# Row maxima of a graph-attention layer gathered and spread by ScalarE copies between partition quarters instead of two TensorE products

## The chip, the core and the metric

The kernel runs on one core of a Trainium2 chip. The core's engines are TensorE (PE: products, and PEld: the loading of their stationary operand), VectorE (DVE), ScalarE (ACT), GpSimd (POOL) and SyncE (SP, which here only issues transfers). Each engine works through its own queue in order; a semaphore holds an instruction until what it needs from another engine is done. The metric is the device time of one execution in microseconds, as the median of the runs.

## The reference

Four graph layers, each followed by a residual sum and a layer norm over the 256 features, on 4096 nodes with a dense 4096 x 4096 matrix `adj`. Layer 0 is masked attention with 4 heads, layers 2 and 3 are normalized products with `adj`. The change lies in layer 1:

```python
Wh = x @ W
e_src = Wh @ a[:d_out]
e_dst = Wh @ a[d_out:]
e = jax.nn.leaky_relu(e_src[:, None] + e_dst[None, :], 0.2)
mask = (adj > 0) | jnp.eye(N, dtype=bool)
e = jnp.where(mask, e, NEG_INF)
alpha = jax.nn.softmax(e, axis=1)
h = alpha @ Wh
x = _layernorm(x + h)
```

For the softmax of a row, the maximum of the row's e is subtracted before the exponential. Since leaky_relu grows with its argument, the maximum of e follows from the maximum of e_dst over the unmasked columns: it is leaky_relu(e_src + that maximum).

## The kernel before

Layer 0 ends near 1440 us; layer 1 runs from there to 1953 us, and layers 2 and 3 follow. Layer 1 takes the rows in 32 units of 128, and each unit in four steps s = 0 to 3 of 32 rows (`NSB` = 4, `QB` = 32). To use all 128 partitions for 32 rows, the 4096 columns are split in `NA` = 4 quarters of 1024 (`QK`): partition a*32 + i holds row i and columns of quarter a. A step works on tiles of 128 x 1024.

The class `Unit` holds what is done for 128 rows:

- `__init__` issues SyncE's loads of the mask (`mk`, two tiles of bfloat16, in a ring of seven) and makes the small tiles `mx` (maxima) and `nm` (the negated, leaky row maximum, the bias of the exponential), each 128 x 4, two buffers. `eq` is e_src, spread to all quarters beforehand.
- `score(s)` (L709, L711), on VectorE: the mask becomes 0 or a large negative number, and one fused instruction adds e_dst (`ed_b`) into z and leaves the maximum of each partition in a column of `mx`. An extra small instruction writes that column.
- `leaky(s)` (L724), on ScalarE: adds e_src and applies the leaky slope, in place.
- `turn_max` and `spread_max`: each row's maximum is spread over four partitions, one per quarter. L730 transposes `mx` on TensorE, L732 takes the maximum over the quarters on VectorE, L739 repeats it four times; L744 turns it back by a product with the identity, and L752 and L755 make `nm`.
- `expo(s)` (L758), on ScalarE: exp(z + nm), in place.
- `turn(s)` (L765), on VectorE: transposes z in 32 x 32 blocks into `pt`, which has two buffers, one per unit.
- `attend(s)` (L775), on TensorE: 16 products of 128 columns of alpha with the matching 128 rows of `wh` (256 features and a column of ones, whose product is the softmax's sum). Each product takes 32 rows of each of the four steps, so a unit's first product needs all four of its `turn`s.
- `finish` (L785, L787 and the layer norm's statistics L113, L114), on VectorE: divides by the sum and adds to the residual row.

The order within each engine's queue is written out by hand in `gat_step(t)`, called for t = 0 to 139. In step t stand, in this order: `score(t)`; where t is a multiple of 4, `turn_max` of the unit that `score` finished in step t-1; `attend(t-10)`; `turn(t-6)`; `spread_max` of the same unit as `turn_max`; `leaky(t)`; `expo(t-5)`; and `finish` of the unit whose last `attend` was in step t-1. So `turn_max` stands in TensorE's queue ahead of the 16 products of that step, and `spread_max` behind them. On VectorE the two halves stand on either side of a `turn`.

The first steps also carry the rest of the projection: `project_w(t+2)` for t = 0 to 5 (16 products, L137, into two PSUM buffers, each emptied by a ScalarE copy, L145), and in step 5 the spreading of e_src of the later rows (`take_es`, L148, then `spread_es`).

Of the kernel before, what the change touches and what calls it, by code (L numbers as in the profile page):

```python
# [8 lines left out]
F32 = mybir.dt.float32  # L9
BF16 = mybir.dt.bfloat16  # L10
AF = mybir.ActivationFunctionType
ALU = mybir.AluOpType
AX = mybir.AxisListType
# [3 lines left out]
P = 128  # L17
# [12 lines left out]
NA = 4  # L30
QB = P // NA
QK = N // NA
NBK = QK // QB
NSB = P // QB
# [6 lines left out]
SLOPE = 0.2  # L41
# [3 lines left out]
def tile_gnn(  # L45
# [18 lines left out]
    nc = tc.nc  # L64
# [10 lines left out]
    ident = const.tile([P, P], F32, name="ident")  # L75
# [35 lines left out]
    def ln_stats(pool, row, ci):  # L111
        st = pool.tile([P, 6], F32, tag="bnst", name="bnst")
        nc.vector.bn_stats(st, row)  # L113
        nc.vector.bn_aggr(mv[:, ci, :], st)  # L114
# [54 lines left out]
    with ExitStack() as l0:  # L169
        ps_t = l0.enter_context(tc.tile_pool(name="l0ps_t", bufs=1, space=PSUM))  # L170
        ps_o = l0.enter_context(tc.tile_pool(name="l0ps_o", bufs=1, space=PSUM))
# [4 lines left out]
        wk = l0.enter_context(tc.tile_pool(name="l0work", bufs=1))  # L176
# [503 lines left out]
    with ExitStack() as l1:  # L680
        wk = l1.enter_context(tc.tile_pool(name="l1work", bufs=2))
        pp_ = l1.enter_context(tc.tile_pool(name="l1pt", bufs=2))
        ps_o = l1.enter_context(tc.tile_pool(name="l1ps_o", bufs=2, space=PSUM))

        class Unit:


            def __init__(self, u):
                self.u = u
                self.z = [None] * NSB  # L690
                self.mk = []
                for half in range(2):
                    mk = bp.tile([P, 2, QK], BF16, tag="bias", name="mk1")
                    i0 = u * P + half * 2 * QB
                    for a in range(NA):
                        nc.sync.dma_start(
                            mk[a * QB : (a + 1) * QB, :, :],
                            edge[i0 : i0 + 2 * QB, a * QK : (a + 1) * QK].rearrange(
                                "(s i) m -> i s m", i=QB
                            ),  # L700
                        )
                    self.mk += [mk[:, 0, :], mk[:, 1, :]]
                self.mx = wk.tile([P, NSB], F32, tag="mx", name="mx")
                self.nm = wk.tile([P, NSB], F32, tag="nm", name="nm")
                self.eq = es_q.rearrange("p a b -> p (a b)")[:, u * NSB : (u + 1) * NSB]

            def score(self, s):
                m = self.mk[s]
                nc.vector.tensor_scalar(m, m, 0.0, MASK1, ALU.is_le, ALU.mult)  # L709
                z = zp.tile([P, QK], F32, tag="z", name="z1")  # L710
                nc.vector.tensor_tensor_reduce(  # L711
                    z,
                    m,
                    ed_b,
                    1.0,
                    NEG,
                    ALU.add,
                    ALU.max,
                    self.mx[:, s : s + 1],
                )  # L720
                self.z[s] = z

            def leaky(self, s):
                nc.scalar.activation(  # L724
                    self.z[s], self.z[s], AF.Prelu, bias=self.eq[:, s : s + 1], alpha=SLOPE
                )

            def turn_max(self):
                pm = ps_o.tile([P, 512], F32, tag="pm", name="pm")
                nc.tensor.transpose(pm[0:NSB, 0:P], self.mx, ident)  # L730
                mr = wk.tile([NSB, QB], F32, tag="mr", name="mr")
                nc.vector.tensor_reduce(  # L732
                    mr,
                    pm[0:NSB, 0:P].rearrange("s (a i) -> s i a", i=QB),
                    AX.X,
                    ALU.max,
                )
                self.mr = wk.tile([NSB, NA, QB], F32, tag="mr4", name="mr4")
                nc.vector.tensor_copy(self.mr, mr.unsqueeze(1).to_broadcast([NSB, NA, QB]))  # L739

            def spread_max(self):

                pm = ps_o.tile([P, 512], F32, tag="pm", name="pm2")
                nc.tensor.matmul(  # L744
                    pm[:, 0:NSB],
                    self.mr.rearrange("s a i -> s (a i)"),
                    ident[0:NSB, 0:NSB],
                    start=True,
                    stop=True,
                )  # L750
                ne = wk.tile([P, NSB], F32, tag="ne", name="ne")
                nc.vector.scalar_tensor_tensor(  # L752
                    ne, pm[:, 0:NSB], -1.0, self.eq, ALU.mult, ALU.subtract
                )
                nc.vector.scalar_tensor_tensor(self.nm, ne, SLOPE, ne, ALU.mult, ALU.min)  # L755

            def expo(self, s):
                nc.scalar.activation(  # L758
                    self.z[s], self.z[s], AF.Exp, bias=self.nm[:, s : s + 1]
                )  # L760

            def turn(self, s):
                if s == 0:
                    self.pt = pp_.tile([P, NBK, NSB, QB], F32, tag="pt", name="pt")
                nc.vector.transpose(  # L765
                    self.pt[:, :, s, :], self.z[s].rearrange("p (b r) -> p b r", r=QB)
                )
                self.z[s] = None

            def attend(self, s):  # L770
                if s == 0:
                    self.po = ps_o.tile([P, 512], F32, tag="po", name="po")
                n = NBK // NSB
                for b in range(s * n, (s + 1) * n):
                    nc.tensor.matmul(  # L775
                        self.po[:, 0 : D + 1],
                        self.pt[:, b, :, :].rearrange("p s i -> p (s i)"),
                        wh[:, b, :],
                        start=(b == 0),
                        stop=(b == NBK - 1),  # L780
                    )

            def finish(self):
                rc = wk.tile([P, 1], F32, tag="rc", name="rc")
                nc.vector.reciprocal(rc, self.po[:, D : D + 1])  # L785
                row = xc[:, self.u, :]
                nc.vector.scalar_tensor_tensor(  # L787
                    row, self.po[:, 0:D], rc, row, ALU.mult, ALU.add
                )
                ln_stats(wk, row, self.u)  # L790

        units = {}
        n_t = NCH * NSB

        def at(t):
            u, s = divmod(t, NSB)
            return (units[u], s) if 0 <= t < n_t else (None, s)

        def gat_step(t):
            if 0 <= t < n_t and t % NSB == 0:  # L800
                units[t // NSB] = Unit(t // NSB)
            u, s = at(t)
            if u:
                u.score(s)
            u, s = at(t - NSB)
            if u and s == 0:
                u.turn_max()
            u, s = at(t - NSB - 6)
            if u:
                u.attend(s)  # L810
            u, s = at(t - NSB - 2)
            if u:
                u.turn(s)
            u, s = at(t - NSB)
            if u and s == 0:
                u.spread_max()
            u, s = at(t)
            if u:
                u.leaky(s)
            u, s = at(t - NSB - 1)  # L820
            if u:
                u.expo(s)
            u, s = at(t - NSB - 7)
            if u and s == NSB - 1:
                u.finish()
                del units[u.u]

        with tc.manual_schedule():
            for t in range(n_t + NSB + 8):
                gat_step(t)  # L830
                if t + 2 < NJ:
                    project_w(t + 2)
                if t + 3 == NJ:
                    take_es(2 * NSB, NBK)
                    spread_es(2 * NSB, NBK, ps_o.tile([P, 512], F32, tag="pm", name="pe"))

                    for j in range(NJ):
                        nc.sync.dma_start(
                            xc.rearrange("p (a j) e -> p a j e", j=NJ)[:, :, j, :],
                            x0.rearrange("(a j p) e -> p a j e", p=P, j=NJ)[:, :, j, :],  # L840
                        )
                    nc.vector.reciprocal(d3, d3)
                    nc.vector.reciprocal(d2, d2)
                    nc.vector.tensor_scalar(sel, sel, -1.0, 1.0, ALU.mult, ALU.add)
                    nc.vector.tensor_tensor(d2, d2, sel, ALU.mult)
# [4 lines left out]
    with ExitStack() as l2:  # L850
# [3 lines left out]
        wk = l2.enter_context(tc.tile_pool(name="l2work", bufs=3))  # L854
# [169 lines left out]
        with tc.manual_schedule():  # L1024
# [4 lines left out]
            for t in range(n_all):  # L1029
# [16 lines left out]
                if c == NP - 1:  # L1046
# [8 lines left out]
                    for s in range(NSJ):  # L1055
                        p = jb * NSJ + s
# [65 lines left out]
```

## Time and profile before

| | us |
|---|---|
| median of 3 runs (2809.99 to 2813.46) | 2810.7 |
| the profiled execution, its own time | 2810.3 |
| its span in the trace | 2808.5 |
| TensorE busy in the span | 2740.4 (98%) |
| VectorE busy | 2234.3 (80%) |
| ScalarE busy | 1615.1 (58%) |
| first attention product of layer 1 (L775) starts at | 1485.5 |
| last one starts at | 1951.9 |

The span is what the trace covers; the run's own time has some 2 us around it. All trace times are counted from the span's start. Of the small instructions on the maxima, each of L730, L732, L739, L752 and L755 occurs 32 times; L744 appears 64 times, as two passes for each product. Their mean durations: L730 272 ns, L732 274 ns, L739 216 ns, L744 258 ns, L752 159 ns, L755 161 ns. A busy time of TensorE is not the same as its full pace: products are pipelined, and one of 379 ns follows the one before by less than that.

### The profile page before, as it was taken

Reading aid. Unit: us, or ns where it says so; the run is one execution under the profiler, and the core shown is the slowest. Engines: PE = TensorE matmul, PEld = TensorE weight load, DVE = VectorE, ACT = ScalarE, POOL = GpSimd, SP = SyncE. Lnnn points to the kernel's source line nnn. Section 1 sums busy time; section 2 is a strip of 40 time slices with the busy share of each in tenths; the row PEclk is TensorE's granted clock in tenths of the full one; section 3 lists DMA queues with packets and bytes.
Section 4 is the critical chain, followed back from the end, with each engine's and each line's share of the span. In section 5 each row is a group of like instructions: output and inputs, shape, how many; then the busy total and the mean of one; then the engine's idle time right before and its main releaser. Section 6 shows DMA issues by size and latency. Waiting matters only on the chain.

```text
span 2808.5 us, 58032 instructions
## 1 busy us (share of the span) xinstructions
PE 2740.4 (98%) x23664; PEld 1870.2 (67%) x23664; DVE 2234.3 (80%) x4091; ACT 1615.1 (58%) x2483; POOL 234.2 (8%) x404
## 2 busy tenths in 40 slices
PE   6999999999999999999998999999999999999997
PEld 4677777777777777777777888887444444444443
DVE  4799999999898999999758888885876568666565
ACT  2699999999999999999855655653100001000000
POOL 1111111111111111111100000000200000000000
PEclk9999999999999999999998999999999999999999
DMA  6344444444444444444362222212555545555552
GB/s 157 61 86 85 87 92 85 88 86 88 90 87 82 90 91 82 86 92 89 100 188 68 76 73 70 76 46 72 177 157 173 163 154 163 164 160 179 180 169 76
DMA packets 671291, 308.01 MB, mean 110 GB/s; under 512 B 547376, under 2 KB 577456, under 8 KB 671024
## 3 DMA queue, kind: packets, MB, share of 16 engines
q1 hardware_dynamic: 655776, 265.10, 38.4%
q0 software_dynamic: 13440, 37.77, 3.5%
q8 instruction: 185, 3.03, 0.5%
q10 hardware_dynamic: 1808, 1.44, 0.2%
q14 instruction: 82, 0.67, 0.1%
HBM read 258.21 MB, written 46.01 MB: 108 GB/s over the span
## 4 chain that ended last, share of the span: by engine, by line
PE 96%; DVE 2%; ACT 1%; DMA 1%; issue 1%; SPq 0%; DVEq 0%; ACTq 0%
PE m L950 27%; PE po L423 17%; PE po L775 16%; PE sc L366 16%; PE ptr L405 10%; PE py L984 2%; PE pq L313 1%; PE pp L335 1%; PE pb L441 1%; PE pk L210 1%; PE pv L226 1%; PE sc L137 1%; PE pm L744 0%; SPq L256 0%; DMA xt<-in_xT 0%
## 5 line engine op out<-in xcount | busy, mean ns | idle before, releaser
L375 DVE CUSTOM_DVE_ANT_0 z<-sc,bias 128x1024 f32<-128x1024 f32 x512 | 605.8, 1220 | 40.5 <-PE sc L366 38.9
L391 ACT ACTIVATE z<-z,nm 128x1024 f32<-128x1024 f32 x512 | 590.2, 1153 | 6.7 <-DVE nm L387 6.7
L413 ACT COPY pt<-ptr 128x1024 f32<-128x1024 f32 x507 | 511.3, 1008 | 99.2 <-PE ptr L405 89.3
L366 PE MATMUL sc<-store,qT 64*128 64x512 f32 x2048 | 507.0, 608 | 1.4 <-DVE mx L375 1.3
L423 PE MATMUL po<-pt,xc 128*64 128x128 f32 x8192 | 504.1, 276 | 0.0
L775 PE MATMUL po<-store,pt 128*128 128x257 f32 x2048 | 459.5, 382 | 3.6 <-DVE pt L765 3.6
L423 PEld LDWEIGHTS po<-pt,xc 128*64 128x64 f32 x8192 | 442.1, 137 | 17.6 <-DVE pt L411 0.2
L405 PEld LDWEIGHTS ptr<-ident,z 64*128 64x128 f32 x8192 | 322.3, 138 | 177.6 <-issue 78.4
L775 PEld LDWEIGHTS po<-store,pt 128*128 128x128 f32 x2048 | 385.0, 190 | 62.9 <-issue 3.6
L950 PE MATMUL m<-asum,ysum 128*128 128x512 f32 x768 | 357.0, 595 | 6.3 <-issue 6.3
L405 PE MATMUL ptr<-ident,z 64*128 64x64 f32 x8192 | 356.5, 225 | 5.8 <-ACT pt L413 4.4
L366 PEld LDWEIGHTS sc<-store,qT 64*128 64x128 f32 x2048 | 192.9, 189 | 119.7 <-issue 109.4
L950 PEld LDWEIGHTS m<-asum,ysum 128*128 128x128 f32 x768 | 146.1, 190 | 177.9 <-issue 160.2
L950 PE MATMUL m<-asum,store 128*128 128x512 f32 x512 | 263.1, 596 | 0.0
L724 ACT ACTIVATE z<-z,es_q 128x1024 f32<-128x1024 f32 x128 | 147.1, 1149 | 183.2 <-DVE mx L711 178.9
L950 PE MATMUL m<-a,ysum 128*128 128x512 f32 x512 | 245.3, 592 | 0.0
L295 POOL DMA_DIRECT2D edge<-mk x256 | 145.3, 568 | 1004.5 <-ACT mk L289 981.0
L956 ACT COPY e<-m 128x512 f32<-128x512 f32 x32 | 18.5, 586 | 351.3 <-PE m L950 351.3
L919 DVE TENSOR_TENSOR asum<-a 128x512 f32<-128x512 f32 x128 | 88.0, 687 | 163.7 <-PE m L950 163.7
L278 DVE SCALAR_TENSOR_TENSOR bias<-rt,gb,u 128x512 f32<-128x512 f32 x256 | 194.1, 758 | 9.1
L950 PEld LDWEIGHTS m<-asum,store 128*128 128x128 f32 x512 | 97.8, 191 | 123.6 <-issue 121.9
L272 DVE STREAM_TRANSPOSE rt<-raw 128x512 f32<-128x512 f32 x256 | 179.6, 702 | 0.0
(126 smaller groups left out, 2544.5 us busy)
## 6 DMA issues: line engine op xcount, KB each, us to landing
a<-in_adjT SPq DMA_DIRECT2D x256, 512.0 KB, 5.1
raw<-in_adjT SPq DMA_DIRECT2D x512, 128.0 KB, 3.9
edge<-mk POOLq DMA_DIRECT2D x256, 128.0 KB, 2.5
mk<-edge SPq DMA_DIRECT2D x256, 128.0 KB, 2.9
xt<-in_xT SPq DMA_DIRECT2D x8, 512.0 KB, 5.3
xq<-in_xT SPq DMA_DIRECT2D x32, 128.0 KB, 3.8
xr<-in_x SPq DMA_DIRECT2D x32, 128.0 KB, 3.0
x<-xs POOLq DMA_DIRECT2D x8, 512.0 KB, 4.0
```

The source lines that it names most:

```text
L272: nc.vector.transpose(rt.rearrange("p (b r) -> p b r", r=QB), self.raw_now[:, half * nb : (half + 1) * nb, :],)
L278: nc.vector.scalar_tensor_tensor(self.bias[k][:, m0 : m0 + HT], rt, gb, u, ALU.mult, ALU.add)
L295: nc.gpsimd.dma_start(edge[self.ib * P : (self.ib + 1) * P, k * TS + m0 : k * TS + m0 + HT], mk)
L366: nc.tensor.matmul(ps[j][:, q * 512 : (q + 1) * 512], self.rows.qT[j * HD : (j + 1) * HD, self.pr, :], kT[j * HD : (j + 1) * HD, self.pr, ...
L375: nc.vector.tensor_tensor_reduce(z, ps[j], self.rows.bias[k], 1.0, NEG, ALU.add, ALU.max, self.mx[:, j, k : k + 1],)
L391: nc.scalar.activation(z, z, AF.Exp, bias=self.nm[:, j : j + 1], accum_out=self.ls[:, j, k : k + 1],)
L405: nc.tensor.transpose(pa[:, r, c, :], z[half, c * P : (c + 1) * P], ident[half, half])
L413: nc.scalar.copy(to, pa)
L423: nc.tensor.matmul(self.po[j * HD : (j + 1) * HD, 0:P], v_sb[:, ci, h * HD : (h + 1) * HD], self.pt[j][k][:, c, :], start=(ci == 0), stop= ...
L724: nc.scalar.activation(self.z[s], self.z[s], AF.Prelu, bias=self.eq[:, s : s + 1], alpha=SLOPE)
L775: nc.tensor.matmul(self.po[:, 0 : D + 1], self.pt[:, b, :, :].rearrange("p s i -> p (s i)"), wh[:, b, :], start=(b == 0), stop=(b == NBK - 1),
L950: nc.tensor.matmul(self.m[i], left, right, start=(c == 0), stop=(c == NP - 1))
```

## The change

`mx` grows from 128 x 4 to 128 x 4 x 4. The maxima of a step still land in its first slot. Then ScalarE copies the three upper quarters' maxima (partitions 32 to 127) into the other slots of partitions 0 to 31 (`gather_max`); VectorE takes the maximum over the four slots and makes `nm` on those 32 partitions alone (`fold_max`); and ScalarE copies `nm` from partitions 0 to 31 to the other three quarters (`spread_max`). The transpose, the product, the PSUM tiles `pm` of both and the repeat of the maximum are gone. In `gat_step` the gather comes ahead of `score`, the fold right behind it, and both halves ahead of `attend` and `turn`; the spread comes last on ScalarE; and `expo(t-5)` now stands before `leaky(t)`. The other product into a `pm` tile, `spread_es` at the start of the layer, stays.

```diff
-                self.mx = wk.tile([P, NSB], F32, tag="mx", name="mx")
+                self.mx = wk.tile([P, NA, NSB], F32, tag="mx", name="mx")
...
-                    self.mx[:, s : s + 1],
+                    self.mx[:, 0, s : s + 1],
...
-            def turn_max(self):
-                pm = ps_o.tile([P, 512], F32, tag="pm", name="pm")
-                nc.tensor.transpose(pm[0:NSB, 0:P], self.mx, ident)
-                mr = wk.tile([NSB, QB], F32, tag="mr", name="mr")
+            def gather_max(self):
+
+                for a in range(1, NA):
+                    nc.scalar.copy(self.mx[0:QB, a, :], self.mx[a * QB : (a + 1) * QB, 0, :])
+
+            def fold_max(self):
+
+                mr = wk.tile([QB, NSB], F32, tag="mr", name="mr")
                 nc.vector.tensor_reduce(
-                    mr,
-                    pm[0:NSB, 0:P].rearrange("s (a i) -> s i a", i=QB),
-                    AX.X,
-                    ALU.max,
-                )
-                self.mr = wk.tile([NSB, NA, QB], F32, tag="mr4", name="mr4")
-                nc.vector.tensor_copy(self.mr, mr.unsqueeze(1).to_broadcast([NSB, NA, QB]))
+                    mr, self.mx[0:QB, :, :].rearrange("p a s -> p s a"), AX.X, ALU.max
+                )
+                ne = wk.tile([QB, NSB], F32, tag="ne", name="ne")
+                nc.vector.scalar_tensor_tensor(
+                    ne, mr, -1.0, self.eq[0:QB, :], ALU.mult, ALU.subtract
+                )
+                nc.vector.scalar_tensor_tensor(
+                    self.nm[0:QB, :], ne, SLOPE, ne, ALU.mult, ALU.min
+                )
 
             def spread_max(self):
 
-                pm = ps_o.tile([P, 512], F32, tag="pm", name="pm2")
-                nc.tensor.matmul(
-                    pm[:, 0:NSB],
-                    self.mr.rearrange("s a i -> s (a i)"),
-                    ident[0:NSB, 0:NSB],
-                    start=True,
-                    stop=True,
-                )
-                ne = wk.tile([P, NSB], F32, tag="ne", name="ne")
-                nc.vector.scalar_tensor_tensor(
-                    ne, pm[:, 0:NSB], -1.0, self.eq, ALU.mult, ALU.subtract
-                )
-                nc.vector.scalar_tensor_tensor(self.nm, ne, SLOPE, ne, ALU.mult, ALU.min)
+                for a in range(1, NA):
+                    nc.scalar.copy(self.nm[a * QB : (a + 1) * QB, :], self.nm[0:QB, :])
...
+            folds, s = at(t - NSB)
+            if s > 0:
+                folds = None
+            if folds:
+                folds.gather_max()
             u, s = at(t)
             if u:
                 u.score(s)
-            u, s = at(t - NSB)
-            if u and s == 0:
-                u.turn_max()
+            if folds:
+                folds.fold_max()
             u, s = at(t - NSB - 6)
             if u:
                 u.attend(s)
             u, s = at(t - NSB - 2)
             if u:
                 u.turn(s)
-            u, s = at(t - NSB)
-            if u and s == 0:
-                u.spread_max()
+            u, s = at(t - NSB - 1)
+            if u:
+                u.expo(s)
             u, s = at(t)
             if u:
                 u.leaky(s)
-            u, s = at(t - NSB - 1)
-            if u:
-                u.expo(s)
+            if folds:
+                folds.spread_max()
```

## The prediction

> **What bounds the kernel now.** I read the page's 40 slices first: the changed code runs in slices 21 to 28 (1447 to 1952 us of 2808.5), where TensorE stands at 8 or 9. Then the busy time by stretch, for layer 1 alone (us, then busy us and count of PE, PEld, DVE, ACT, POOL; granted clock; DMA):
>
> ```profile
> 1474.00:1478.00 4.00, 0.00 (x0) 0.00 (x0) 3.93 (x8) 2.19 (x2) 0.00 (x0) 0.50 0.00 0
> 1490.00:1494.00 4.00, 4.00 (x18) 3.43 (x17) 2.42 (x4) 3.46 (x4) 0.00 (x0) 0.88 0.46 139
> 1738.00:1752.53 14.53, 14.53 (x69) 12.34 (x68) 12.69 (x25) 8.75 (x9) 0.00 (x0) 1.00 0.24 74
> ```
>
> One unit of 128 rows (last line) takes 14.53 us: TensorE never rests, VectorE works 12.69 us, ScalarE 8.75. The DMA queues have room. A busy PE can still be a late PE, so the chain of waits comes next (start, us, what):
>
> ```profile
> 1702.74 10.63 PE po L775 x48
> 1713.48 3.48 PE po L775 x16
> 1717.27 10.63 PE po L775 x48
> ...
> 1906.21 10.63 PE po L775 x48
> 1920.74 31.52 PE po L775 x144
> ```
>
> The end is set by the attention products of L775, unit after unit, and the period is (1906.21 - 1702.74)/14 = 14.534 us. The holes after each 48 and each 16 are the transpose of L730 and the product of L744. The timeline of one unit shows what they do:
>
> ```profile
> 1712.99 0.08 PEld L730 LDWEIGHTS pm<-ident,mx 128*4 128x4 f32 x1
> 1713.21 0.27 PE L730 MATMUL pm<-ident,mx 128*4 128x128 f32 x1
> ...
> 1714.11 0.27 DVE L732 TENSOR_REDUCE mr<-pm 4x32 f32<-4x128 f32 x1
> ...
> 1714.42 0.22 DVE L739 COPY mr<-mr 4x128 f32<-4x128 f32 x1
> 1714.56 1.23 DVE L765 STREAM_TRANSPOSE pt<-z 128x1024 f32<-128x1024 f32 x1
> ...
> 1716.89 0.38 PE L744 MATMUL pm<-ident,mr 4*128 4x4 f32 x2
> ...
> 1717.31 0.16 DVE L752 SCALAR_TENSOR_TENSOR ne<-pm,es_q 128x4 f32<-128x4 f32 x1 [1.53 <-PE pm L744]
> ```
>
> VectorE stands 1.53 us in every unit because L744 is queued behind 16 products of L775. Its 12.69 busy and these 1.53 make 14.22 of 14.53: VectorE is held by TensorE, not the reverse. It isn't far behind, though: the last of a unit's four transposes ends at 1720.35 and TensorE's next unit begins about 0.3 us later (16 products after 1717.20). So I must also ask whether VectorE stays ahead once TensorE is faster. The tail shows what a unit costs TensorE with neither L730 nor L744 in it:
>
> ```profile
> 1938.37 0.17 DVE L785 RECIPROCAL rc<-po 128x1 f32<-128x1 f32 x1 [7.97 <-PE po L775]
> ...
> 1952.28 0.17 DVE L785 RECIPROCAL rc<-po 128x1 f32<-128x1 f32 x1 [12.55 <-PE po L775]
> ```
>
> Both waited for the last product of a unit; between them lie exactly 64 products of L775: 13.91 us, or 0.2173 us each.
>
> **What the Trainium skill says.** "ScalarE: Activation LUTs", section "What ACT_TABLE_LOAD costs", prices an instruction with immediate scale and bias at 186 ns + 0.833 ns per element and says that instructions back to back overlap by about 93 ns. Four elements then make an estimate of 0.19 us, 0.10 to 0.19 in a row; the trace agrees in size, with 0.20 us for a 128x2 square root (L610). Its section "Table sets: the hidden batching unit" says copy is in every set; the trace agrees, since layer 0 mixes 507 copies of L413 with exponentials without loads between. "TensorE: Matmul & The Clock Gate", section "What's actually happening", says the clock falls to half after an idle window of about 3.4 us and returns after a busy one, with windows that don't start with the kernel: the 0.50 and 0.88 above agree. "VectorE: DVE Perf Modes", section "Two Vector instructions with no wait between them", has an instruction held when its start quadrant differs from the one before. The new VectorE instructions all start at partition 0, like their neighbours, so I charge nothing for that; no run so far shows a changed quadrant.
>
> **The change part by part.**
>
> *TensorE loses L730 and L744 in each of 32 units.* A unit in the loop costs 14.534, one without them 13.91, so the pair costs 0.62 us, filling and draining included (the holes in the chain show 0.11 and 0.31; the rest sits in the stretched products beside them). Units 0 and 1 have theirs before the first attention product at 1485.5; 30 lie in the stretch where TensorE is the bound. 30 x 0.62 = 18.6 us off the path.
>
> *VectorE* loses L732 (0.27) and L739 (0.22), two small operations on 128 partitions (0.16 each) and the 1.53 us wait. It gains a reduction of 32x16 to 32x4 and two operations on 32x4: by L387 (0.16, 128x8) and L755 (0.16) about 0.48. Its busy time goes from 12.69 to about 12.4, at most 12.7 if narrow operations cost no less. It has room in 13.91.
>
> *ScalarE gains six copies of 32x4.* I take 0.2 us each, 1.2 in a unit, bounds 0.1 and 0.4 (0.4 is twice the nearest row). 8.75 + 1.2 = 10.0 of 13.91. Gather: its three copies need the last maximum of step t-1, and stand on ScalarE behind the leaky of that step (1.15), which needs the same maximum. From that maximum they end at 0.1 + 1.15 + 0.6 = 1.9 us. VectorE meanwhile does a transpose (1.16), the mask (0.42) and the fused add-and-max (1.16), 2.74 us from start to start; so the fold finds them done, with 0.8 to spare (0.2 at 0.4 per copy). Behind a late fold would stand turn and the next score, and for these TensorE waits. Spread: it is issued after leaky of step t, which starts with the maximum of that step and lasts 1.15; the fold is done 0.5 after that. So spread doesn't wait either, ends about 1.9 us after the maximum, and exp of the unit's first quarter ends near 3.1. That quarter is turned two steps later, over 5 us from there.
>
> *The order on ScalarE: exp goes ahead of leaky.* Same instructions; exp needs nothing of the current step and now fills the time in which ScalarE waited for the score (178.9 us in all for L724). Leaky is read five steps later. I cost it at nothing; the idle 4 us per unit are its cover.
>
> *What is late next.* VectorE is no longer tied to TensorE by L752 and runs ahead until the transposes of unit u must wait for the products of unit u-2 (two buffers of pt). From that moment T it needs transpose 1.16, finish 1.26, steps of 2.74, 2.74 + 0.5 and 2.74 until the fourth transpose is done: 11.2 us. TensorE needs it at T + 13.91. Slack 2.7 us in place of 0.3, so TensorE has no gap.
>
> *Start of layer 1.* Here VectorE and TensorE wait on each other through the removed products:
>
> ```profile
> 1461.48 0.28 DVE L732 TENSOR_REDUCE mr<-pm 4x32 f32<-4x128 f32 x1 [6.19 <-PE pm L730]
> ...
> 1462.37 7.22 PE L137 MATMUL sc<-w_sb,xt 128*128 128x257 f32 x32
> ...
> 1471.24 0.18 DVE L148 COPY esd<-store 128x24 f32<-128x24 f32 x1 [6.80 <-ACT store L145]
> ```
>
> TensorE stops 1.1 us between 1461.2 and 1462.4 for the first unit's pair, and the projections behind it move by as much; ScalarE's last copies (L145) now come behind table load, exp and leaky as before, in another order, with 1.2 us of small copies before them. Following ScalarE's queue with the trace's durations the last copy ends near 1470.0 in place of 1471.2: gain 1.2, plus 0.2 for the shorter fold of unit 1: 1.4 us. Bounds 0 (the small copies eat it) and 3 (the first products catch an earlier clock window, 1.7 us more: one window of 3.4 at half speed).
>
> Sum: 18.6 + 1.4 = 20.0. The profiled execution took 2810.3 us (span 2808.5), which is 0.4 below the median 2810.7. 2810.3 - 20.0 = 2790.3 us. Layers 0, 2 and 3 aren't touched.
>
> **The rivals.**
> (a) *Part of it is given back.* A gap stays at each unit's edge, from the wait for pt or from ScalarE's round trip when a copy takes 0.4 or more. For: VectorE was only 0.3 us ahead. Against: the slack just counted. If a third is lost, 20 - 7 = 13: 2797 us.
> (b) *The wait only changes its name.* L752's wait becomes a wait of the fold for the gather copies. VectorE holds TensorE only when wait and busy time exceed 13.91, from 1.4 us of wait; for no change it would take 2.0, that is gather copies of about 1.1 us each. Then about 2810.
> (c) *Slower: ScalarE becomes the bound.* Place: the six copies between quarters, a case that the trace never shows (all its ScalarE rows have output and input on the same partitions). Deciding point: (13.91 - 8.75)/6 = 0.86 us per copy; the old period is reached at 0.96. At 1.1 us per copy, as if each waited for the pipe to empty beside a 1.15 us neighbour, ScalarE needs 15.35 per unit, 0.82 over the old period, 30 x 0.82 = 25 us: about 2835. Against: no small row on ScalarE is above 0.23.
> (d) *It doesn't do what it says*: were the copies put on another engine or TensorE still asked, the row counts would show it. The diff issues them as scalar copies; I give this nothing apart from (b).
>
> **How the numbers follow.** Forecast 0.79, (a) 0.10, (b) 0.04, (c) 0.07. The forecast's own range is 2787 (a clock window gained, 3 in place of 1.4, and the other estimates a little low) to 2793 (no gain at the start, copies at 0.4 costing a little). To leave out no more than 2 in 10 the range reaches into (a): 2786.5 to 2797. A change of 0.2% is 5.6 us, about what a measurement here tells from none. Forecast and (a) are faster by more: 0.89; (b) is the same, 0.04; (c) slower, 0.07.
>
> **What would show it.** Right: rows L730 and L744 gone; the chain of L775 without holes and 13.9 us from unit to unit; six ScalarE copies of 32x4 near 0.2 us; no wait of the fold on ScalarE; a new VectorE wait of about 1 us per unit for TensorE (L765 or L785); first L775 near 1484. Wrong: a unit longer than 14.1, gaps of PE before L775 released by VectorE's pt, copies above 0.4 us, or ScalarE near 9 tenths in slices 21 to 28.

## The result, and the profile after

The changed kernel takes 2790.27 us (median of 4 runs, 2787.91 to 2790.96) against 2810.61 us before (median of 4): a ratio of 0.992 with a 95% interval of 0.9908 to 0.9933. The profiled execution took 2790.52 us, its span 2788.7 us, 19.8 less than before. L770 is now the attention product, L760 the transpose into `pt`, L753 the exponential, L780 the start of `finish`; L731 and L750 are the copies of the gather and the spread, L736, L740 and L743 the fold.

The chain of waits of the changed kernel in layer 1 (start, us, what) has one piece where there was one for every 48 or 16 products:

```profile
1471.56 12.64 issue
1484.20 447.22 PE po L770 x2048
1931.44 0.18 DVE rc L780
```

("Issue" is time for which the profile names no releaser. The first unit's fourth transpose ends at 1484.10 us, and TensorE starts 0.1 us later.) The holes are gone. From one unit's first product to the next unit's it is 13.91 us, as in the tail of the kernel before. The busy time by stretch for one such unit (us, then busy us and count of PE, PEld, DVE, ACT, POOL; clock; DMA) and the waits between 1550 and 1850 us (us in total, times, longest):

```profile
1738.00:1751.91 13.91, 13.91 (x65) 12.11 (x64) 12.41 (x25) 10.01 (x14) 0.00 (x0) 1.00 0.25 77
```

```profile
ACT z L724 <- DVE mx L711: 76.7, 44, 3.1
DVE pt L760 <- PE po L770: 26.2, 22, 1.2
```

VectorE does 12.41 us of work per unit and ScalarE 10.01. The wait for L744 is replaced by one for the products that still read the old `pt`, 26.2/22 = 1.19 us a unit, and no wait of the fold is in the list. The timeline of the round trip shows why:

```profile
1699.02 0.08 DVE L711 DVE_READ_ACCUMULATOR2_ANT mx<- 128x1 f32 x1
1699.02 1.24 DVE L760 STREAM_TRANSPOSE pt<-z 128x1024 f32<-128x1024 f32 x1
1699.14 1.15 ACT L724 ACTIVATE z<-z,es_q 128x1024 f32<-128x1024 f32 x1 [3.08 <-DVE mx L711]
...
1700.30 0.60 ACT L731 COPY mx<-mx 32x4 f32<-32x4 f32 x3
1700.60 1.23 DVE L711 CUSTOM_DVE_ANT_0 z<-mk,ed_b 128x1024 f32<-128x1024 bf16 x1
...
1701.75 0.16 DVE L736 TENSOR_REDUCE mr<-mx 32x4 f32<-32x16 f32 x1
...
1703.12 0.60 ACT L750 COPY nm<-nm 32x4 f32<-32x4 f32 x3
```

The last maximum is there at 1699.1. The gather stands behind one leaky and ends at 1700.90; VectorE asks for it at 1701.75, 0.85 us later. Three copies between quarters take 0.60 us, 192 ns each.

### The profile page after: what moved, and what is told of

Its sections match the earlier page's. It is cut to its first block, busy times and chain, and to the rows that moved or that the text cites. A ratio compares the mean times of both kernels' runs of the same rounds, so it can differ in the third digit from the quotient of the medians.

```text
span 2788.7 us, 57962 instructions
## 1 busy us (share of the span) xinstructions
PE 2720.9 (98%) x23568; PEld 1862.4 (67%) x23568; DVE 2225.5 (80%) x4059; ACT 1655.4 (59%) x2675; POOL 234.3 (8%) x404
## 4 chain that ended last, share of the span: by engine, by line
PE 93%; issue 3%; DVE 1%; DMA 1%; ACT 1%; SPq 0%; POOL 0%; DVEq 0%; POOLq 0%; ACTq 0%
PE m L948 27%; PE po L423 17%; PE po L770 16%; PE sc L366 16%; PE ptr L405 10%; PE py L982 2%; PE pq L313 1%; PE pp L335 1%; PE pb L441 1%; PE pk L210 1%; PE pv L226 1%; DMA mk<-edge 1%; SPq L256 0%; DMA x<-xs 0%; DVE z L375 0%
## 5 line engine op out<-in xcount | busy, mean ns | idle before, releaser
L770 PE MATMUL po<-store,pt 128*128 128x257 f32 x2048 | 447.2, 380 | 12.6 <-issue 12.6
L770 PEld LDWEIGHTS po<-store,pt 128*128 128x128 f32 x2048 | 388.6, 190 | 70.9 <-issue 12.7
L724 ACT ACTIVATE z<-z,es_q 128x1024 f32<-128x1024 f32 x128 | 146.5, 1145 | 120.5 <-DVE mx L711 111.9
L760 DVE STREAM_TRANSPOSE pt<-z 128x1024 f32<-128x1024 f32 x128 | 158.1, 1237 | 41.7 <-PE po L770 41.7
```

Source lines behind the costliest of these rows:

```text
L724: nc.scalar.activation(self.z[s], self.z[s], AF.Prelu, bias=self.eq[:, s : s + 1], alpha=SLOPE)
L760: nc.vector.transpose(self.pt[:, :, s, :], self.z[s].rearrange("p (b r) -> p b r", r=QB))
L770: nc.tensor.matmul(self.po[:, 0 : D + 1], self.pt[:, b, :, :].rearrange("p s i -> p (s i)"), wh[:, b, :], start=(b == 0), stop=(b == NBK - 1),
```

## The experiments

The theory: TensorE bounds layer 1, and what it spends on the pair L730 and L744 is what the change gives, with a little at the layer's start. The rivals: it was VectorE's wait of 1.53 us; it was the new order of exp and leaky. After these the room that is left was measured, then the price of each half of the pair, then the start of the layer. Every run stands beside runs of the kernel before on its own chip (2809.5 to 2810.7 us). Periods are from the start of a unit's first product to that of the next unit.

**1. The order alone,** on the kernel before:

```diff
+            u, s = at(t - NSB - 1)
+            if u:
+                u.expo(s)
             u, s = at(t)
             if u:
                 u.leaky(s)
-            u, s = at(t - NSB - 1)
-            if u:
-                u.expo(s)
```

> The kernel before with one part of the change alone: exp of step t-5 stands ahead of leaky of step t on ScalarE. TensorE still carries the pair of L730 and L744. Theory (TensorE's time for the pair is the gain): 2810.6 us, within 2 us, unit period 14.53. Rival (the order on ScalarE gives the gain or part of it): 2791 us if all of it, 2800 if half.

Measured: 2809.63 us, ratio 1.0 (0.9991 to 1.0009), period 14.53. The order gives nothing by itself.

**2. The pair put back, without a wait,** into the changed kernel, around the products of the step:

```diff
+            if folds:
+                pm = ps_o.tile([P, 512], F32, tag="pm", name="pm")
+                nc.tensor.transpose(pm[0:NSB, 0:P], ident[:, 0:NSB], ident)
             u, s = at(t - NSB - 6)
             if u:
                 u.attend(s)
+            if folds:
+                pm = ps_o.tile([P, 512], F32, tag="pm", name="pm2")
+                nc.tensor.matmul(
+                    pm[:, 0:NSB], ident[0:NSB, :], ident[0:NSB, 0:NSB], start=True, stop=True
+                )
```

> The changed kernel with the two TensorE instructions put back in their old places, on the identity and read by nobody: no engine waits for them, and VectorE and ScalarE work as in the changed kernel. Theory (TensorE's time for the pair is the gain): unit period 14.53 again, 30 x 0.62 = 18.6 us lost, so 2809 us (the start may keep 0 to 1.5 us). Rival (VectorE's wait of 1.53 us per unit for L744 was what cost): 2790 us, since that wait stays gone. Between: the share of each.

Measured: 2808.81 us, ratio 0.9995 (0.9986 to 1.0004), period 14.53. The whole gain is given back though VectorE works as in the changed kernel. The chain of this run has the holes again, and the list of waits shows that VectorE only waits longer for TensorE (36.3/20 = 1.8 us a unit):

```profile
1613.45 0.31 PE pm L815 x2
1613.76 10.63 PE po L770 x48
1624.39 0.11 PE pm L809
1624.50 3.48 PE po L770 x16
```

```profile
DVE pt L760 <- PE po L770: 36.3, 20, 1.8
```

VectorE's wait was a sign of TensorE's load, not a cost. The rival falls, and with the first run so does the other.

**3. More work on VectorE:** the last transpose of each unit is done twice.

```diff
-                nc.vector.transpose(
-                    self.pt[:, :, s, :], self.z[s].rearrange("p (b r) -> p b r", r=QB)
-                )
+                for _ in range(2 if s >= 3 else 1):
+                    nc.vector.transpose(
+                        self.pt[:, :, s, :], self.z[s].rearrange("p (b r) -> p b r", r=QB)
+                    )
```

> The changed kernel with the fourth transpose of each unit done twice on VectorE: 1.16 us more VectorE work per unit, no wait more. Theory (TensorE is the bound, VectorE has 1.19 us of waiting per unit): 2790 us, and up to 2793 as the room is just used up; the wait of VectorE's transpose for TensorE falls from 1.19 to about 0. Rival (VectorE sets the period, and the gain came from its removed wait): 30 x 1.16 = 35 us slower, 2825 us.

Measured: 2791.14 us (2790.99 to 2792.44), period 13.91, and no wait of VectorE for TensorE is left between 1550 and 1850 us. The room was real and is now used up.

**4. The old order kept in the changed kernel:** leaky again ahead of exp, spread last.

```diff
-            u, s = at(t - NSB - 1)
-            if u:
-                u.expo(s)
             u, s = at(t)
             if u:
                 u.leaky(s)
+            u, s = at(t - NSB - 1)
+            if u:
+                u.expo(s)
             if folds:
                 folds.spread_max()
```

> The changed kernel with leaky of step t ahead of exp of step t-5 on ScalarE again, spread still last. Theory (order costs nothing either way): 2790 us, within 2 us. Rival (the new order is needed so that the copies find ScalarE free): spread and with it exp come later, VectorE's transposes wait for exp, 2795 us or more.

Measured: 2790.16 us (2787.77 to 2793.36). The reordering isn't needed: VectorE's wait for TensorE is 20.3/21 = 0.97 us a unit in place of 1.19, so the later copies, for which the fold now waits 0.2 us, take that from a room that nobody uses.

**5. The last two transposes doubled** (`s >= 2` in the edit of the third run).

> The changed kernel with the third and the fourth transpose of each unit done twice on VectorE: 2.32 us more work per unit. Theory (TensorE is the bound up to 1.19 us more on VectorE, from there VectorE): VectorE's own time per unit is 13.91 - 1.19 + 2.32 = 15.04 us, the period becomes that, 30 x 1.13 = 34 us, 2824 us. Rival (there is more room than the wait shows, as waits elsewhere shrink too): under 2815 us.

Measured: 2827.52 us, period 15.19 (15.04 expected). VectorE is the bound, and TensorE stops at each unit's edge:

```profile
1700.63 14.15 PE L771 MATMUL po<-store,pt 128*128 128x257 f32 x64 [1.04 <-DVE pt L761]
...
1709.16 2.50 DVE L761 STREAM_TRANSPOSE pt<-z 128x1024 f32<-128x1024 f32 x2
```

The expectation was 0.15 us low because a repeat costs about 1.25 us and not the 1.16 of a transpose before another instruction: 13.91 - 1.19 + 2 x 1.25 = 15.2. In the trace the repeat carries a wait on VectorE's own semaphore; it overwrites what the first one wrote.

**6. and 7. The gather made longer:** its three copies repeated four and seven times.

```diff
-                for a in range(1, NA):
+                for a in list(range(1, NA)) * 4:
```

> The changed kernel with the gather done four times over, 12 copies in place of 3, 1.85 us more on ScalarE ahead of the fold. Theory (the fold had 0.83 us to spare, and VectorE 1.19 us of waiting behind it): the fold now waits about 1.0 us for the copies, VectorE's wait for TensorE shrinks by as much, the time stays: 2790 us, up to 2792. Rival (a late fold goes straight into the period): 30 x 1.0 = 30 us slower, 2820 us.

Measured: 2793.66 us, period 13.91. The fold now waits, and the wait takes the place of the one for TensorE, at no cost per unit:

```profile
DVE mr L736 <- ACT mx L731: 23.5, 22, 1.1
```

The 3.4 us more are lost at the start of the layer: from the first leaky (L724) to the first product it is 39.3 us in place of 35.0. The first two units' gathers have nine copies more each, which at 0.205 us a copy would be 3.7 us, an estimate; the clock may have the rest, as 0.59 was granted between 1467 and 1471 us, where the changed kernel had 1.00.

> The changed kernel with the gather done seven times over, 21 copies, 3.7 us more on ScalarE. Theory: the fold waits 2.9 us, 1.7 more than VectorE has to give, so the period is 12.72 + 2.9 = 15.6 us and the time 30 x 1.7 = 52 us longer, 2842 us; ScalarE is busy 13.6 of 15.6 us and isn't the bound. Rival (ScalarE's busy time sets the end, not the place of the copies): period 13.9, no more than 2795 us.

Measured: 2849.16 us, ratio 1.0135 (1.0118 to 1.0152), period 15.74. In the stretch of one unit ScalarE works 13.34 of 15.74 us and VectorE 12.41, so neither is full; what sets the period is the fold's wait in the middle of VectorE's queue:

```profile
1700.00:1715.74 15.74, 14.16 (x65) 12.03 (x64) 12.41 (x24) 13.34 (x33) 0.00 (x0) 1.00 0.21 67
```

```profile
1708.49 0.17 DVE L736 TENSOR_REDUCE mr<-mx 32x4 f32<-32x16 f32 x1 [3.02 <-ACT mx L731]
```

12.72 us of VectorE's own and 3.02 of wait are 15.74. The expectation had 15.6, with copies of 0.205 us; 21 of them took 4.52, 0.215 each. The 7 us over the expected 2842 are again the start: it is 44.1 us to the first product, 9.1 more than in the changed kernel. The stretch from the first to the last product is 51.0 us longer (52 expected), and layers 2 and 3 happen to be 1.5 us shorter.

**8. The transpose alone, and 9. the product alone,** each the second run without the other half.

> The kernel of e2_pair_unread with the transpose alone put back, not the product. Theory (each costs what stands around its hole in the chain): 0.62 us of the pair splits into about 0.22 for the transpose and 0.40 for the product (two passes), so 30 x 0.22 = 6.6 us over the changed kernel, 2797 us. Rival (the interruption costs, whatever interrupts): half of 18.6, 2799.5 us.

Measured: 2791.86 us, period 14.02: 0.11 us a unit. The split that was expected is wrong.

> The kernel of e2_pair_unread with the 4-row product alone, without the transpose. e10_transpose_only left the transpose 0.11 us per unit, not 0.22. Theory (the two add up): 0.51 us per unit, period 14.42, 30 x 0.51 = 15 us over the changed kernel, 2805.5 us. Rival (either alone is cheap and the two together hinder each other): period under 14.3, less than 2802 us.

Measured: 2804.35 us, period 14.42: 0.51 us a unit. The two add to 0.62. The chains of the two runs, transpose first:

```profile
1605.60 13.91 PE po L770 x64
1619.51 0.11 PE pm L809
```

```profile
1611.94 14.11 PE po L770 x64
1626.05 0.31 PE pm L812 x2
```

The transpose leaves the 64 products at 13.91 us and costs its hole. The product costs its hole of 0.31 and stretches the products around it by 0.20.

**10. The start of the layer:** the spreading of e_src two steps later, on the changed kernel.

```diff
-                if t + 3 == NJ:
+                if t + 1 == NJ:
                     take_es(2 * NSB, NBK)
```

> The changed kernel with the spreading of e_src (take_es, spread_es and what stands with them) two steps later, after step 7 in place of step 5, ahead of step 8, the first whose leaky reads it. Theory (at the start VectorE loses some 5 us waiting for ScalarE's last projection copies, with scores and transposes queued behind that wait): the first attention product starts about 3 us earlier, near 1481, and the time falls by 3 us, 1 in 1000: 2787 us. Rival (something else holds the first product, such as the exponentials behind the table load): first product within 0.5 us of 1484.2, time unchanged at 2790 us.

Measured: 2785.35 us, ratio to before 0.9911 (0.9896 to 0.9926). The intervals of this ratio and of the changed kernel's overlap, so the times alone don't tell the two apart. The traces do: from the first leaky to the first product it is 31.7 us in place of 35.0, and the first product starts at 1480.1. In the changed kernel VectorE stood still ahead of take_es:

```profile
DVE esd L148 <- ACT store L145: 5.2, 1, 5.2
```

With the step moved, scores and transposes go on meanwhile. The forecast of 3 us fits the 3.3 us at the start. The medians differ by 4.9, and the rest lies elsewhere: in this trace layer 0 ended 0.8 us earlier, and the products and layers 2 and 3 took 0.9 us less. It is the fastest version with a cause that the trace shows.

**11. and 12. An early table load,** on top of the tenth:

```diff
+            early = wk.tile([P, 1], F32, tag="early", name="early")
+            nc.scalar.activation(early, ones_col, AF.Exp)
             for t in range(n_t + NSB + 8):
```

> The kernel of e8_es_late with one tiny exponential on ScalarE at the start of layer 1, where ScalarE waits 4.3 us for e_src. Its table load of 1.28 us then doesn't stand between the spread of unit 0 and its first exponential any more. Theory (ScalarE's queue is the chain to the first product, as the chain of waits of e8_es_late shows): first product 1.3 us earlier, near 1478.8, time 1.3 us less, about 2784 us, too little to tell by the times alone. Rival (TensorE's projections hold ScalarE's last copies): no change in the first product's time.

Measured: 2784.91 us, and 31.7 us to the first product, as without it. The exponential ran at 1362.1 us, in layer 0, ahead of the square roots, so the load stayed at its place: the edit didn't do what it was for. The twelfth run lets it read `ed_b[:, QK - 1 : QK]` instead.

> As e9_early_exp, whose tiny exponential went into layer 0, ahead of the square roots, and so moved no table load; here it reads the last column of e_dst, so that it can't run before layer 1 begins, and the load of 1.28 us falls into ScalarE's 4.3 us wait for e_src. Theory (ScalarE's queue is the chain to the first product): from the start of the first leaky to the first product 1.3 us less than in e8_es_late, the time about 2784 us. Rival (the projections hold the last copies): no change.

Measured: 2784.85 us. Now the load ran at 1445.6 us, in ScalarE's wait, and the first product still comes 32.0 us after the first leaky. The rival holds for the larger part: with the load gone from its place, ScalarE's last copy waits for TensorE's projection,

```profile
1469.73 0.59 ACT L145 COPY store<-sc 128x514 f32<-128x514 f32 x1 [0.78 <-PE sc L137]
```

so that `take_es` comes 22.7 us after the first leaky in place of 23.2: of 1.28 us, 0.5 are left. `spread_es` (L155) then takes 1.87 us in place of 1.04, as it falls into a stretch of half clock, and the 0.5 are gone too. What is taken out of one engine's part of a chain shortens the chain only as far as the next engine's work allows.

## Why the prediction was right

**TensorE's pair, 18.6 us.** It holds in kind and size: 14.53 to 13.91 us a unit, and the second run puts it back. Of the trace's difference, the stretch from the first to the last attention product is 466.36 us before and 446.83 after, 19.5 less; 30 x 0.62 of it are the pair.

**The start, 1.4 us.** From the first leaky to the first product it was 36.6 us and is 35.0: 1.6. The first product was forecast near 1484 and came at 1484.2. VectorE waits 7.3 us there for the first gather behind ScalarE's projection copies, longer than it waited for L730 (6.2), and it doesn't matter, as ScalarE's last copies come 1.0 us earlier (take_es at 1470.19 in place of 1471.24).

**What the sum didn't have.** Three terms of about 1 us or less cancel. The half clock ends 3 us earlier, and the first products meet less of it: between 1486 and 1490 us the granted clock is 0.76 in place of 0.50, between 1490 and 1494 it is 1.00 in place of 0.88, and 446.83 is 0.9 less than 466.36 - 18.7. Layers 2 and 3 take 851.0 us from their first product on in place of 850.0. The clock shows there too, in the last rows, where less is granted in a like stretch, before and then after:

```profile
2788.00:2798.00 10.00, 6.16 (x21) 4.52 (x20) 7.60 (x19) 2.09 (x5) 0.00 (x0) 0.84 0.00 0
```

```profile
2768.00:2778.00 10.00, 6.67 (x18) 4.70 (x17) 6.94 (x17) 1.90 (x4) 0.00 (x0) 0.66 0.00 0
```

The other runs agree: eleven of the fourteen traces meet the same stretches of half clock in these layers up to the last rows. In six of them, after among these, the last rows then have one of 3.4 us and one of 6.8, and the layers take 850.9 to 851.1 us; in five, before among these, they have two of 3.4, and it is 849.8 to 850.4. And layer 0 ended 0.2 us later in this execution. 18.7 + 1.6 + 0.9 - 1.0 - 0.2 = 20.0, against 19.8 in the spans, the rest being rounding. The forecast was also counted from the profiled execution: the medians differ by 20.3. The agreement to a tenth of a microsecond is therefore partly chance.

That the clock's windows don't start with the kernel, as "TensorE: Matmul & The Clock Gate" has it in "What's actually happening", agrees with these traces. Layer 0 has the same code in all of them, and yet in one stretch of it the kernel before was granted 0.98 and the first run 0.51:

```profile
98.00:104.00 6.00, 4.73 (x62) 2.86 (x61) 5.14 (x8) 4.73 (x9) 1.29 (x2) 0.98 0.34 54
```

```profile
98.00:104.00 6.00, 4.90 (x37) 2.97 (x37) 4.00 (x7) 4.21 (x7) 1.14 (x2) 0.51 0.34 53
```

**VectorE and ScalarE as covers.** The work came out as summed: VectorE 12.41 us a unit (12.4), ScalarE 10.01 (10.0), a copy 0.19 us (0.2), the fold 0.85 us ahead of need (0.8). The estimate of 0.19 us for such a copy, from the price in "ScalarE: Activation LUTs", "What ACT_TABLE_LOAD costs", agrees with the trace. The overlap of 93 ns of instructions back to back that the same section names doesn't show in these short copies, as three took 0.60 us. Crossing quarters cost nothing extra, so rival (c) had no ground. The slack of 2.7 us came out too. From the release of `pt`, the moment T, to the end of a unit's fourth transpose it is 11.1 us, for 11.2 in the sum:

```profile
1695.03 1.25 DVE L760 STREAM_TRANSPOSE pt<-z 128x1024 f32<-128x1024 f32 x1 [1.19 <-PE po L770]
...
1704.93 1.24 DVE L760 STREAM_TRANSPOSE pt<-z 128x1024 f32<-128x1024 f32 x1
```

**The step that was off** is the point from which rival (b) decides. It was put at 1.4 us of wait, from busy time (with the forecast's own 12.4 us it would be 1.5). VectorE loses about 0.3 us a unit between instructions, so its own time is 12.72 us and the room 1.19. The runs with the doubled transposes and the long gathers fix it: 1.1 us of fold wait is free, 3.0 us costs 1.8. It changed nothing in the forecast, as the fold didn't wait. A small slip of the sum is of the same kind: with 0.4 us a copy the fold would have had 0.3 us to spare, not 0.2.

**Rival (a)** didn't occur: no gap remains at a unit's edge, where a gap would have come from `pt`.

## What to carry to other kernels

Before pricing an instruction that leaves the bounding engine, find a stretch of the same trace where that engine runs without it: the last unit of the tail gave 0.62 us, where the holes in the chain showed 0.42. A wait on an engine that isn't the bound is no gain to be had; put the load back without the wait, and the time tells. And count the room of a covering engine from start to start, with its waits taken out, not from its busy time.

## What the runs showed of the hardware

A transpose of 128x4 among products of full height cost TensorE 0.11 us. A product with 4 rows of contraction, 4x128 by 4x4 in two passes, cost 0.51, nearly five times as much, though its moving operand has 4 columns where the transpose's has 128. The weight loads of the second run show an idle 0.33 us ahead of each such product, and nothing of the kind ahead of the transpose:

```profile
1711.22 0.08 PEld L809 LDWEIGHTS pm<-ident 128*4 128x4 f32 x1
...
1715.11 0.29 PEld L815 LDWEIGHTS pm<-ident 4*128 4x128 f32 x2 [0.33 <-issue]
```

The load of the transpose begins together with the product ahead of it (1711.22 us), as the loads of L770 do; that of the 4-row operand begins 0.31 us after that product began (1714.81), when most of it is over. Why, whether for the number of rows or the number of passes, wasn't tried and stays open.
